# A GCN and a sparse GAT layer on one core: mask bytes in eight row tables in place of mask bits in four, with list rounds and x tiles placed elsewhere

## The chip, the cores and the metric

The kernel runs on one core of one Trainium2 chip. The metric is the device time of one execution in microseconds. Before the change it is 2188.02 us, the median of three runs (2182.11 to 2196.11).

## The reference

There are 4096 nodes with 512 features, all fp32, and a weighted adjacency matrix `adj` in which under one per cent of the entries are non-zero. Two layers are computed, each with a layer norm and a ReLU in front and a residual around it:

```python
# layer 0
h = max(layernorm(x), 0)
d = rowsum(adj) ** -0.5                      # 0 where the sum isn't positive
x = x + relu((d[:, None] * adj * d[None, :]) @ h @ W + b)
# layer 1
h = max(layernorm(x), 0)
g = h @ W1
e = leaky_relu((g @ a[:512]) + (g @ a[512:]).T, 0.2)
pos = softmax(where(adj > 0, e, -1e12), axis=1)
neg = -softmax(where(adj > 0, -e, -1e12), axis=1)
x = x + elu(concat([pos @ h, neg @ h], axis=1) @ wtrans)
```

Layer 1 needs of `adj` only where it is positive: a mask of 4096 x 4096.

## The kernel before

**Layer 0, first pass.** The 4096 source nodes are 32 tiles j of 128 rows. For each j the kernel loads the rows of `adj` (four loads of 512 KB), sums them on ScalarE (ACT) and VectorE (DVE), normalizes the tile of x, turns it by four TensorE (PE) transposes and a copy to `hx_t` (`turn_x`), multiplies it with W (`project`) and scales it to `y0[j]`, which stays in SBUF (`scale`). At the same time it multiplies the first group of six target tiles, 26 to 31, with the `y0[j]` that is there. `turn_x` for tile j + 2 runs in the middle of the matmuls of tile j, and `project` for tile j + 1 stands before those matmuls.

**Layer 0, groups.** Target tiles are handled in groups, `GROUPS`, of which the first is that of the first pass; seven follow, called b = 1 to 7 here: four target tiles each, and two in the last. A group loads tiles `at` of the transposed adjacency (`load_at`, on the queue of SyncE, SP, four buffers), multiplies them with `y0` (`multiply`, line 718) in 16 steps jp of two source tiles each, and accumulates in PSUM. The accumulators of the previous group are taken up at the start of the next (`finish0`, the epilogue).

**Mask bits.** Each tile `at` also passes through `pack` on DVE: line 627 makes of each element either a power of two or zero, line 639 sums 16 of them to a 16-bit word, line 644 reduces the words to a flag for each pair of a source node and a block of 64 targets. Words are kept in SBUF (`words`) until a whole slice of a table is there; then GpSimd (POOL) writes them with one DMA (line 654). Two groups, (24, 2) and (12, 4), are packed ahead of their time with extra loads of their `at` tiles through the same four buffers (`EARLY`): in b = 2, and in b = 4 and 5.

**Epilogue.** For each of its tiles `finish0` computes the layer's output, writes it to DRAM (`x1_dram`), normalizes it to a row `h` (two buffers) and writes `h` with its attention term to four tables in DRAM, two writes on ACT's queue and two on POOL's. There are four tables because each holds, next to the row of every source node, the mask of that node for a quarter of the targets. At its end the attention terms `s_all` are scattered to DRAM and broadcast back to all partitions (`s_bc`), on ACT's queue (lines 693 and 697).

**Lists.** For each block of 64 targets the kernel lists the source nodes with at least one edge into it. DVE finds them in rounds of eight (`list_round`, MAX8 and MATCH_REPLACE8, lines 372 and 374); POOL joins the parts by indirect DMAs (line 387), and SP loads the joined lists as `idx` (`deal`, line 399). The steps of this are queued in `listing`, and the group loop takes two of them in each step jp, and four from b = 6 on.

**Layer 1.** For each of 32 pairs of blocks (128 targets) POOL gathers 22 chunks of 128 table rows (line 861), in three tiles of 8, 6 and 8 chunks; a block of 64 targets uses two of the three. `weights` computes for block r the sums z of both attention terms (line 882), picks the bits of the mask out of the gathered words (line 890), takes the leaky ReLU (899), two exponentials on ACT (902), multiplies them by the mask (903), and sums them. `product` multiplies with the gathered rows (934), and `finish1` applies wtrans (967). The first gathers read the third of the four tables.

The Tile framework places instructions by readiness as well as by program order, except where `keep_in_program_order` (the argument `pin`) holds them.

Of the kernel before, what the change touches and what calls it, by code (L numbers as in the profile page):

```python
# [19 lines left out]
P = 128  # L20
# [9 lines left out]
RB = 64  # L30
WB = 16
NE = 8
CAPS = (168, 144, 168)
NTAB = 4
CHUNKS = (8, 6, 8)
ROW_T = 512
ROW_W = 516
ROW = 548
MAXS = 40.0
# [217 lines left out]
def gcn_gat_kernel(  # L257
# [37 lines left out]
    STR = LEN + 2 * P  # L295
    WPR = RB // WB
    RPT = NR // NTAB
    LOFF = (0, CAPS[0], CAPS[0] + CAPS[1])

# [25 lines left out]

    wts = const.tile([P, WB], U16, name="wts")
    for k in range(WB):
        nc.gpsimd.memset(wts[:, k : k + 1], 1 << k)
    base = const.tile([P, 1], F32, name="base")
# [46 lines left out]
    def table_rows(g, c, lst):  # L376

        li = const.tile([P, CAPS[c]], I32, tag=f"li{c}", name=f"li{g}_{c}")
# [36 lines left out]
    with tc.tile_pool(name="y0", bufs=1) as y_pool, tc.tile_pool(  # L415
# [39 lines left out]
        xs, hx_t, ars, parts, y0 = {}, {}, {}, {}, {}  # L455
        words, packed = {}, {}

# [100 lines left out]
        def turn_x(ln_pool, j, pin=False):  # L558

            hx = ln_pool.tile([P, F], F32, tag="hx", name=f"hx{j}", bufs=2)  # L560
            normalize(hx, xs.pop(j), f"a{j}", pin)
            tp = bank(f"tx{j}")
            for c in range(FC):
                i = nc.tensor.transpose(
                    tp[:, c * P : (c + 1) * P], hx[:, c * P : (c + 1) * P], ident
                )
                if pin:
                    tc.keep_in_program_order(i)
            hx_t[j] = ln_pool.tile([P, F], F32, tag="hx_t", name=f"hx_t{j}")
            nc.vector.tensor_copy(hx_t[j], tp)  # L570
# [47 lines left out]
        def pack(i0, j0, at, pin=False):  # L618

            nj, w = at.shape[1], at.shape[2] // WB  # L620
            g, w0 = i0 * P // (N // NTAB), i0 * P % (N // NTAB) // WB
            if g not in words:
                words[g] = bits_pool.tile(
                    [P, NJ, RPT * WPR], U16, tag="words", name=f"words{g}", bufs=3
                )
            m = bits_pool.tile([P, nj * w, WB], U16, tag="m", name=f"m{i0}_{j0}")
            i = nc.vector.scalar_tensor_tensor(  # L627
                m,
                at.rearrange("p c (w k) -> p (c w) k", k=WB),
                0.0,  # L630
                wts[:, :].unsqueeze(1).to_broadcast([P, nj * w, WB]),
                ALU.is_gt,
                ALU.mult,
            )
            if pin:
                tc.keep_in_program_order(i)
            wd = words[g][:, j0 : j0 + nj, w0 : w0 + w]
            with nc.allow_low_precision("sums of different powers of two below 2**16 are exact"):
                nc.vector.tensor_reduce(  # L639
                    wd, m.rearrange("p (c w) k -> p c w k", c=nj), AX.X, ALU.add  # L640
                )
            e, k = j0 // EJ, j0 % EJ
            half, r = i0 // (NJ // 2), i0 % (NJ // 2) * 2
            nc.vector.tensor_reduce(  # L644
                flags[half].rearrange("p (k e) b -> p k e b", e=NE)[
                    :, k : k + nj, e, r : r + w // WPR
                ],
                wd.rearrange("p c (b w) -> p c b w", w=WPR),
                AX.X,
                ALU.max,  # L650
            )
            packed[g, e] = packed.get((g, e), 0) + nj * w
            if packed[g, e] == EJ * RPT * WPR:
                nc.gpsimd.dma_start(  # L654
                    out=rows_of(g, e)[:, :, ROW_W : ROW_W + RPT * WPR // 2],
                    in_=words[g][:, e * EJ : (e + 1) * EJ, :].bitcast(I32),
                )

        def finish0(work, i0, acc):
# [8 lines left out]
            for j, y in enumerate(ys, i0):  # L668
# [14 lines left out]
                e, k = j // EJ, j % EJ  # L683
                for g in (2, 3, 0, 1):
                    (nc.scalar, nc.gpsimd)[g % 2].dma_start(
                        out=rows_of(g, e)[:, k, :ROW_W], in_=h.bitcast(I32)
                    )
                dot(0, s_all[:, j : j + 1])
                nc.vector.tensor_copy(t_all[:, j : j + 1], h[:, ROW_T : ROW_T + 1])

            n = len(acc)
# [35 lines left out]
        with tc.tile_pool(name="w0", bufs=1) as w0_pool, tc.tile_pool(  # L727
# [23 lines left out]
            for j in range(NJ):  # L751
# [38 lines left out]
        with tc.tile_pool(name="work0", bufs=2) as work:  # L790
            for b, (i0, n) in enumerate(GROUPS[1:], 1):
                acc = None
                for jp in range(NJ // 2):
# [20 lines left out]
                pending = (i0, acc)  # L814
            finish0(work, *pending)


# [25 lines left out]
    def sparse_layer1():  # L843
        with tc.tile_pool(name="wt", bufs=1) as wt_pool, tc.tile_pool(
# [31 lines left out]
            def weights(r):  # L876

                nk = sum(CHUNKS[r % 2 : r % 2 + 2])
                z = tmp.tile([P, nk, RB], F32, tag="z", name=f"z{r}")
                m = tmp.tile([P, nk, RB], U16, tag="m1", name=f"m1_{r}")  # L880
                for gt, k, n in parts(r):
# [4 lines left out]
                        ALU.add,  # L886
                    )
                    w = gt[:, :, ROW_W:].bitcast(U16)
                    w = w[:, :, (r % RPT) * WPR : (r % RPT + 1) * WPR]
                    nc.vector.tensor_tensor(  # L890
                        m[:, k : k + n].rearrange("p k (w c) -> p k w c", c=WB),
                        w.unsqueeze(3).to_broadcast([P, n, WPR, WB]),
                        wts[:, :].unsqueeze(1).unsqueeze(1).to_broadcast([P, n, WPR, WB]),
                        ALU.bitwise_and,
                    )
                p = p_pool.tile([P, nk, 2, RB], F32, tag="p", name=f"p{r}")
                for k, n in ((0, nk),) if r not in first else tuple((k, n) for _, k, n in parts(r)):
                    zk = z[:, k : k + n]
                    nc.vector.scalar_tensor_tensor(zk, zk, ALPHA, zk, ALU.mult, ALU.max)  # L899
                    for g in range(2):  # L900
                        e = p[:, k : k + n, g, :]
                        nc.scalar.activation(e, zk, AF.Exp, scale=(1.0, -1.0)[g])  # L902
                        nc.vector.scalar_tensor_tensor(  # L903
                            e, m[:, k : k + n], 0.0, e, ALU.is_gt, ALU.mult
                        )
                half = nk // 2
# [145 lines left out]
```

## Time and profile before

| | us |
|---|---|
| median of three runs | 2188.02 |
| the profiled execution | 2204.95 |
| its span, first to last instruction | 2203.1 |
| PE busy | 2076.8 |
| DVE busy | 1273.7 |
| POOL busy | 963.5 |
| last matmul of layer 0, start | 1096.52 |
| first gather of layer 1, start | 1109.60 |
| first product of layer 1, start | 1131.50 |

The profile shows one execution. Durations of instructions come from the engines; a matmul's end is modelled, and since matmuls are pipelined a row of them reads as busy even where each takes longer than it must. Each fp32 matmul is two instructions in the counts. "Idle before" a group of instructions is the time its engine stood still just before them, and the name behind the arrow is what ended it. The granted clock of PE is given as a share of full speed. The DMA share is the mean busy share of the 16 DMA engines.

### The profile page before, as it was taken

The numbers are of one execution on the slowest core, as the hardware profiler recorded it, in microseconds if no ns is written. First come the engines' busy times: TensorE is split into PE (matmuls) and PEld (weight loads), VectorE is DVE, ScalarE is ACT, GpSimd is POOL, SyncE is SP. The second block draws the span as 40 slices with busy tenths as digits, with TensorE's granted clock in tenths as the row PEclk, the third lists the DMA queues.
The fourth block names the chain that finished last, engine by engine and source line by source line (L and its number), as shares of the span: only waits on it lengthen the run. The fifth ranks groups of instructions, "written<-read, shape, count | busy, mean of one in ns | idle before, by whom it ended". The sixth has DMA issues, their size and how long they took to land.

```text
span 2203.1 us, 16742 instructions
## 1 busy us (share of the span) xinstructions
PE 2076.8 (94%) x5184; PEld 936.5 (43%) x5184; DVE 1273.7 (58%) x2559; ACT 407.5 (18%) x745; POOL 963.5 (44%) x1009
## 2 busy tenths in 40 slices
PE   7998999999998898999846999999999999999998
PEld 3443444434443343444323444444444444444443
DVE  6665537465899866587235545555554555555451
ACT  5555511000000000000011212122211212221221
POOL 2000002021102231102267777777777777777750
PEclk9999999999999999999968999999999999999999
DMA  9899728273735447452586777777777776777750
GB/s 350 320 345 323 290 69 256 79 210 113 216 88 181 123 145 198 152 152 88 153 257 196 202 214 207 210 208 212 206 207 214 212 212 198 210 212 205 218 162 21
DMA packets 172825, 431.59 MB, mean 196 GB/s; under 512 B 39091, under 2 KB 48307, under 8 KB 172726
## 3 DMA queue, kind: packets, MB, share of 16 engines
q0 software_dynamic: 72144, 243.76, 38.5%
q1 hardware_dynamic: 84112, 164.75, 23.2%
q10 hardware_dynamic: 16470, 21.92, 3.0%
q8 instruction: 42, 0.69, 0.1%
q14 instruction: 57, 0.47, 0.1%
HBM read 376.67 MB, written 53.67 MB: 195 GB/s over the span
## 4 chain that ended last, share of the span: by engine, by line
PE 42%; POOL 3%; issue 2%; DMA 2%; DVE 1%; ACT 0%; DVEq 0%; another core or an unknown queue 0%; POOLq 0%
PE u L934 32%; PE o L967 9%; POOL g L861 3%; PE tp L952 1%; DMA table<-h 1%; DMA g<-table,idx 1%; DMA wt_sb<-in_wtrans 0%; PE cs L923 0%; DVE p L903 0%; DVE z L882 0%; DVE z L899 0%; DVE m L890 0%; DVE total L912 0%; DVE eo L979 0%; DVE eo L975 0%
## 5 line engine op out<-in xcount | busy, mean ns | idle before, releaser
L718 PE MATMUL acc<-y,at 128*128 128x512 f32 x2048 | 903.8, 598 | 34.4 <-DMA at<-in_adj_t 34.2
L861 POOL DMA_INDIRECT g<-table,idx x704 | 796.4, 1131 | 231.4 <-issue 197.7
L934 PE MATMUL u<-g,p 128*128 128x512 f32 x1792 | 792.6, 599 | 28.8 <-DMA g<-table,idx 24.7
L718 PEld LDWEIGHTS acc<-y,at 128*128 128x128 f32 x2048 | 389.0, 192 | 519.6 <-issue 470.9
L934 PEld LDWEIGHTS u<-g,p 128*128 128x128 f32 x1792 | 337.5, 191 | 433.5 <-issue 420.5
L882 DVE TENSOR_TENSOR z<-g,s_bc 128x512 f32<-128x512 f32 (+1 forms) x128 | 80.2, 627 | 456.3 <-DMA g<-table,idx 401.6
L627 DVE SCALAR_TENSOR_TENSOR m<-at,wts 128x1024 uint16<-128x1024 f32 (+2 forms) x144 | 157.8, 1098 | 162.7 <-DMA at<-in_adj_t 162.4
L967 PE MATMUL o<-wt_sb,ut 128*128 128x512 f32 x512 | 226.0, 593 | 2.6 <-issue 2.0
L902 ACT ACTIVATE p<-z 128x896 f32<-128x896 f32 (+2 forms) x132 | 115.1, 919 | 515.1 <-issue 418.3
L639 DVE TENSOR_REDUCE words<-m 128x64 uint16<-128x1024 uint16 (+2 forms) x144 | 157.4, 1095 | 2.2
L903 DVE SCALAR_TENSOR_TENSOR p<-m,p 128x896 f32<-128x896 uint16 (+2 forms) x132 | 134.5, 1060 | 26.4 <-ACT p L902 15.1
L967 PEld LDWEIGHTS o<-wt_sb,ut 128*128 128x128 f32 x512 | 94.7, 190 | 111.0 <-issue 110.3
L595 PE MATMUL yp<-w_sb,hx_t 128*128 128x512 f32 x256 | 122.6, 624 | 19.0 <-DVE flags L644 6.4
L548 ACT ACTIVATE rrb<-rrb 128x1 f32<-128x1 f32 x32 | 6.1, 198 | 668.9 <-DVE rrb L547 447.2
L387 POOL DMA_INDIRECT ld<-li,off x48 | 47.0, 978 | 183.5 <-DVE li L380 89.2
L654 POOL DMA_DIRECT2D table<-words x32 | 24.5, 766 | 224.3 <-DVE flags L644 142.9
L585 ACT ACTIVATE ar<-ar 128x1024 f32<-128x1024 f32 x96 | 100.7, 1050 | 49.9 <-DMA ar<-in_adj 49.4
L556 POOL DMA_DIRECT2D xt<-in_x x28 | 15.3, 547 | 205.8 <-ACT hx L552 99.3
L943 ACT ACTIVATE us<-u,rl 128x512 f32<-128x512 f32 x64 | 43.9, 686 | 246.1 <-issue 118.8
L595 PEld LDWEIGHTS yp<-w_sb,hx_t 128*128 128x128 f32 x256 | 49.5, 199 | 89.3 <-issue 73.0
L912 DVE TENSOR_TENSOR total<-total 128x384 f32<-128x384 f32 (+2 forms) x192 | 81.9, 427 | 2.3
L372 DVE MAX8 lst<-keys 128x8 f32<-128x512 f32 x120 | 79.6, 680 | 0.8
(122 smaller groups left out, 1115.7 us busy)
## 6 DMA issues: line engine op xcount, KB each, us to landing
ar<-in_adj SPq DMA_DIRECT2D x128, 512.0 KB
at<-in_adj_t SPq DMA_DIRECT2D x120, 512.0 KB
table<-h ACTq DMA_DIRECT2D x64, 258.0 KB
table<-h POOLq DMA_DIRECT2D x64, 258.0 KB
at<-in_adj_t SPq DMA_DIRECT2D x32, 384.0 KB
g<-table,idx POOLq DMA_INDIRECT x704
xr<-in_x POOLq DMA_DIRECT2D x32, 256.0 KB
x1d<-y POOLq DMA_DIRECT2D x32, 256.0 KB
```

The costliest lines, as they stand in the source:

```text
L585: i = nc.scalar.activation(ar, ar, AF.Identity, accum_out=part[:, c : c + 1])
L595: nc.tensor.matmul(yp, hx_t[j][:, c * P : (c + 1) * P], w0_sb[:, c, :], start=c == 0, stop=c == FC - 1,)
L627: i = nc.vector.scalar_tensor_tensor(m, at.rearrange("p c (w k) -> p (c w) k", k=WB), 0.0, wts[:, :].unsqueeze(1).to_broadcast([P, nj * w, ...
L639: nc.vector.tensor_reduce(wd, m.rearrange("p (c w) k -> p c w k", c=nj), AX.X, ALU.add)
L718: nc.tensor.matmul(a, at[:, c, it * P : (it + 1) * P], y0[j0 + c], start=j0 + c == 0, stop=j0 + c == NJ - 1,)
L861: nc.gpsimd.indirect_dma_start(out=gt[:, k, :], out_offset=None, in_=table[2 * n // RPT], in_offset=bass.IndirectOffsetOnAxis(ap=idx[n // ...
L882: nc.vector.tensor_tensor(z[:, k : k + n], gt[:, :, ROW_T : ROW_T + 1].bitcast(F32).to_broadcast([P, n, RB]), s_bc[r // 8][:, r % 8 * RB : ...
L902: nc.scalar.activation(e, zk, AF.Exp, scale=(1.0, -1.0)[g])
L903: nc.vector.scalar_tensor_tensor(e, m[:, k : k + n], 0.0, e, ALU.is_gt, ALU.mult)
L912: nc.vector.tensor_tensor(total[:, :n], total[:, :n], total[:, half - n : half], ALU.add)
L934: nc.tensor.matmul(u, p[:, k0 + k].rearrange("p g c -> p (g c)"), gt[:, k, :F].bitcast(F32), start=k0 + k == 0, stop=k0 + k == nk - 1,)
L967: nc.tensor.matmul(po, ut[:, g, c, :], wt_sb[:, g * FC + c, :], start=g == 0 and c == 0, stop=g == 1 and c == FC - 1,)
```

## The change

The mask is kept as one byte for each element. `pack` becomes one comparison that writes bytes and one reduction that reads them as 32-bit words for the flags; the byte tile, four source tiles deep and in two buffers, is the source of the DMA to the table, with no `words` in between. Since a mask of bytes is eight times as large, there are eight tables, each with the mask for an eighth of the targets (512 bytes in each row; a row has 644 words of 4 bytes, before 548), and `finish0` writes `h` eight times: six writes on ACT's queue and two on POOL's. In layer 1 the multiplication by the mask reads the bytes in the gathered row, separately for the two gathered tiles, and the picking of bits goes.

The scatter and broadcast of the attention terms become a function of their own, `spread_s`, on SP's queue, called at step 6 of the next group (for the last group, after its epilogue). The lists take no step in jp 0 to 2 of the groups up to b = 6; later they take two, in b = 6 four, and in b = 7 one in each jp. In the first pass `turn_x` handles tile j + 3 in the matmuls of tile j, from j = 0 on, with four buffers of `hx_t`.

```diff
-NTAB = 4
+NTAB = 8
-ROW = 548
+ROW = 644
...
-            hx_t[j] = ln_pool.tile([P, F], F32, tag="hx_t", name=f"hx_t{j}")
+            hx_t[j] = ln_pool.tile([P, F], F32, tag="hx_t", name=f"hx_t{j}", bufs=4)
...
-            nj, w = at.shape[1], at.shape[2] // WB
-            g, w0 = i0 * P // (N // NTAB), i0 * P % (N // NTAB) // WB
-            if g not in words:
-                words[g] = bits_pool.tile(
-                    [P, NJ, RPT * WPR], U16, tag="words", name=f"words{g}", bufs=3
-                )
-            m = bits_pool.tile([P, nj * w, WB], U16, tag="m", name=f"m{i0}_{j0}")
-            i = nc.vector.scalar_tensor_tensor(
-                m,
-                at.rearrange("p c (w k) -> p (c w) k", k=WB),
-                0.0,
-                wts[:, :].unsqueeze(1).to_broadcast([P, nj * w, WB]),
-                ALU.is_gt,
-                ALU.mult,
-            )
+            nj, w = at.shape[1:]
+            e, k = j0 // EJ, j0 % EJ
+            if k == 0:
+                masks[i0] = bits_pool.tile([P, EJ, w], U8, tag="m", name=f"m{i0}_{j0}")
+            m = masks[i0][:, k : k + nj]
+            i = nc.vector.tensor_scalar(m, at, 0.0, None, ALU.is_gt)
...
-                nc.vector.tensor_reduce(
-                    wd, m.rearrange("p (c w) k -> p c w k", c=nj), AX.X, ALU.add
-                )
...
-                wd.rearrange("p c (b w) -> p c b w", w=WPR),
+                m.bitcast(I32).rearrange("p c (b w) -> p c b w", w=RB // 4),
...
+            if k + nj == EJ:
+                for t in range(i0 // TT, (i0 + w // P - 1) // TT + 1):
+                    a, b = max(i0, t * TT), min(i0 + w // P, (t + 1) * TT)
+                    nc.gpsimd.dma_start(
+                        out=rows_of(t, e)[
+                            :, :, ROW_W + (a - t * TT) * P // 4 : ROW_W + (b - t * TT) * P // 4
+                        ],
+                        in_=masks[i0][:, :, (a - i0) * P : (b - i0) * P].bitcast(I32),
+                    )
...
-                for g in (2, 3, 0, 1):
-                    (nc.scalar, nc.gpsimd)[g % 2].dma_start(
+                for n, g in enumerate((4, 5, 6, 7, 0, 1, 2, 3)):
+                    (nc.scalar, nc.scalar, nc.gpsimd)[n % 3].dma_start(
...
-            nc.scalar.dma_start(out=sd.rearrange("(k p) -> p k", p=P), in_=s_all[:, i0 : i0 + n])
+            nc.sync.dma_start(out=sd.rearrange("(k p) -> p k", p=P), in_=s_all[:, i0 : i0 + n])
...
-                nc.scalar.dma_start(
+                nc.sync.dma_start(
                     out=s_bc[j // 4][:, j % 4 * P : (j % 4 + k) * P],
...
-                turn = partial(turn_x, ln_pool, j + 2, j < 3) if 0 < j < NJ - 2 else None
+                turn = partial(turn_x, ln_pool, j + 3, j < 2) if j < NJ - 3 else None
...
+                    if jp == 6:
+                        spread_s(pending[0], len(pending[1]))
...
-                    for _ in range(2 if b < 6 else 4):
+                    for _ in range((2, 4, 1)[max(b - 5, 0)] if jp > 2 or b > 6 else 0):
...
-                        ALU.bitwise_and,
...
-                        nc.vector.scalar_tensor_tensor(
-                            e, m[:, k : k + n], 0.0, e, ALU.is_gt, ALU.mult
-                        )
+                for gt, k, n in parts(r):
+                    m = gt[:, :, ROW_W:].bitcast(U8)[:, :, r % RPT * RB : (r % RPT + 1) * RB]
+                    for g in range(2):
+                        e = p[:, k : k + n, g, :]
+                        nc.vector.scalar_tensor_tensor(e, m, 0.0, e, ALU.is_gt, ALU.mult)
```

More of the change, by code (lines that the diff above doesn't have):

```diff
@@ L30 @@
 RB = 64
-WB = 16
 NE = 8
 CAPS = (168, 144, 168)
-NTAB = 4
+NTAB = 8
 CHUNKS = (8, 6, 8)
@@ L295, in gcn_gat_kernel @@
     STR = LEN + 2 * P
-    WPR = RB // WB
     RPT = NR // NTAB
+    TT = RPT * RB // P
     LOFF = (0, CAPS[0], CAPS[0] + CAPS[1])
@@ L324, in gcn_gat_kernel @@
     s_bc = [const.tile([P, 4 * P], F32, name=f"s_bc{k}") for k in range(NJ // 4)]
-    wts = const.tile([P, WB], U16, name="wts")
-    for k in range(WB):
-        nc.gpsimd.memset(wts[:, k : k + 1], 1 << k)
     base = const.tile([P, 1], F32, name="base")
@@ L376, in table_rows @@
     def table_rows(g, c, lst):
-        li = const.tile([P, CAPS[c]], I32, tag=f"li{c}", name=f"li{g}_{c}")
+        li = list_pool.tile([P, CAPS[c]], I32, tag=f"li{c}", name=f"li{g}_{c}")
         src = lst[:, LOFF[c] : LOFF[c] + CAPS[c]]
@@ L455, in gcn_gat_kernel @@
         xs, hx_t, ars, parts, y0 = {}, {}, {}, {}, {}
-        words, packed = {}, {}
+        masks = {}
         def make_keys(g):
@@ L618, in pack @@
         def pack(i0, j0, at, pin=False):
-            nj, w = at.shape[1], at.shape[2] // WB
-            g, w0 = i0 * P // (N // NTAB), i0 * P % (N // NTAB) // WB
-            if g not in words:
-                words[g] = bits_pool.tile(
-                    [P, NJ, RPT * WPR], U16, tag="words", name=f"words{g}", bufs=3
-                )
-            m = bits_pool.tile([P, nj * w, WB], U16, tag="m", name=f"m{i0}_{j0}")
-            i = nc.vector.scalar_tensor_tensor(
-                m,
-                at.rearrange("p c (w k) -> p (c w) k", k=WB),
-                0.0,
-                wts[:, :].unsqueeze(1).to_broadcast([P, nj * w, WB]),
-                ALU.is_gt,
-                ALU.mult,
-            )
+            nj, w = at.shape[1:]
[4 more added lines that the diff above has]
+            i = nc.vector.tensor_scalar(m, at, 0.0, None, ALU.is_gt)
             if pin:
                 tc.keep_in_program_order(i)
-            wd = words[g][:, j0 : j0 + nj, w0 : w0 + w]
-            with nc.allow_low_precision("sums of different powers of two below 2**16 are exact"):
-                nc.vector.tensor_reduce(
-                    wd, m.rearrange("p (c w) k -> p c w k", c=nj), AX.X, ALU.add
-                )
-            e, k = j0 // EJ, j0 % EJ
             half, r = i0 // (NJ // 2), i0 % (NJ // 2) * 2
@@ L645, in pack @@
                 flags[half].rearrange("p (k e) b -> p k e b", e=NE)[
-                    :, k : k + nj, e, r : r + w // WPR
+                    :, k : k + nj, e, r : r + w // RB
                 ],
-                wd.rearrange("p c (b w) -> p c b w", w=WPR),
+                m.bitcast(I32).rearrange("p c (b w) -> p c b w", w=RB // 4),
                 AX.X,
@@ L651, in pack @@
             )
[L652 to L656, printed above, removed]
-                )
+            if k + nj == EJ:
[7 more added lines that the diff above has]
+                    )
         def finish0(work, i0, acc):
@@ L689, in finish0, with spread_s @@
                 nc.vector.tensor_copy(t_all[:, j : j + 1], h[:, ROW_T : ROW_T + 1])
-            n = len(acc)
+        def spread_s(i0, n):
             sd = s_dram[i0 * P : (i0 + n) * P]
-            nc.scalar.dma_start(out=sd.rearrange("(k p) -> p k", p=P), in_=s_all[:, i0 : i0 + n])
+            nc.sync.dma_start(out=sd.rearrange("(k p) -> p k", p=P), in_=s_all[:, i0 : i0 + n])
             j = i0
@@ L814, in gcn_gat_kernel @@
                 pending = (i0, acc)
+            while listing:
+                listing.pop(0)()
             finish0(work, *pending)
+            spread_s(pending[0], len(pending[1]))
         ok = small.tile([P, 8], F32, tag="ok", name="ok", bufs=1)
@@ L879, in weights @@
                 z = tmp.tile([P, nk, RB], F32, tag="z", name=f"z{r}")
-                m = tmp.tile([P, nk, RB], U16, tag="m1", name=f"m1_{r}")
                 for gt, k, n in parts(r):
@@ L886, in weights @@
                         ALU.add,
[L887 to L893, printed above, removed]
-                        ALU.bitwise_and,
                     )
@@ L902, in weights @@
                         nc.scalar.activation(e, zk, AF.Exp, scale=(1.0, -1.0)[g])
-                        nc.vector.scalar_tensor_tensor(
-                            e, m[:, k : k + n], 0.0, e, ALU.is_gt, ALU.mult
-                        )
+                for gt, k, n in parts(r):
[3 more added lines that the diff above has]
+                        nc.vector.scalar_tensor_tensor(e, m, 0.0, e, ALU.is_gt, ALU.mult)
                 half = nk // 2
```

## The prediction

> **What bounds the kernel now.** I read the busy shares first, then the windows cut at the matmuls that open each group, then the waits of PE, VectorE (DVE) and SP in each, and last the chain of waits.
>
> ```profile
> PE 2076.8 (94%) x5184; PEld 936.5 (43%) x5184; DVE 1273.7 (58%) x2559; ACT 407.5 (18%) x745; POOL 963.5 (44%) x1009
> ```
>
> Cut at the changes of stage, the windows give 332 us for the first pass (group 26 to 31), 765 for the seven other groups, 78 for the passage to layer 1, 1028 for layer 1. In layer 1 PE is busy 1012.9 of 1028, and the chain is PE alone: one node block takes 32.2 us (product starts at 1245.23, 1277.45, 1309.68). Only the first 1175 us can be shortened. The groups, in order (columns: stretch, length, PE, PEld, DVE, ACT, POOL busy with counts, clock, DMA share, GB/s):
>
> ```profile
> 332.07:441.94 109.87, 109.87 (x257) 48.64 (x256) 63.40 (x125) 5.99 (x12) 14.36 (x31) 1.00 0.55 170
> 441.94:560.60 118.66, 112.59 (x257) 48.74 (x256) 68.86 (x132) 4.07 (x8) 19.12 (x34) 0.99 0.57 158
> 560.60:671.78 111.18, 111.18 (x283) 49.56 (x284) 107.30 (x230) 3.85 (x8) 16.37 (x27) 1.00 0.48 139
> 671.78:799.08 127.30, 113.43 (x257) 48.65 (x256) 102.39 (x190) 3.85 (x8) 34.09 (x45) 0.99 0.51 153
> 799.08:924.05 124.97, 114.78 (x258) 50.22 (x257) 75.44 (x123) 3.96 (x8) 15.67 (x30) 0.95 0.60 168
> 924.05:1035.15 111.10, 111.10 (x284) 49.48 (x283) 99.57 (x256) 3.73 (x8) 20.24 (x33) 1.00 0.46 137
> 1035.15:1096.52 61.37, 57.12 (x128) 24.98 (x127) 13.10 (x46) 3.85 (x8) 18.37 (x30) 0.94 0.56 155
> ```
>
> Group b=1 loses nothing: 109.87 us for 257 matmuls, 0.4275 each. Against that b=2, 4, 5 lose 8.8, 17.4, 15.1 us, b=3 and 6 1.3 and 1.2, b=7 (half a group: 54.9) 6.4: together 50. The losers b=2, 4, 5 are the groups that also load and pack an EARLY group through the same four `at` buffers, so their prefetch reaches about two steps, 13.7 us, not four, 27. All their PE gaps end on "DMA at<-in_adj_t". The worst come just after an epilogue. For b=2:
>
> ```profile
> 468.00:470.00 2.00, 2.00 (x6) 0.92 (x5) 2.00 (x3) 0.00 (x0) 0.26 (x2) 1.00 0.97 293
> 472.00:474.00 2.00, 2.00 (x6) 0.93 (x5) 0.00 (x0) 0.00 (x0) 0.00 (x0) 1.00 0.95 44
> 476.00:478.00 2.00, 0.44 (x2) 0.00 (x0) 0.00 (x0) 0.00 (x0) 0.00 (x0) 1.00 0.64 53
> 480.00:484.00 4.00, 2.90 (x4) 1.31 (x5) 2.92 (x4) 0.00 (x0) 0.00 (x0) 0.68 0.50 111
> ```
>
> The DMA share stays high while the rate falls from 293 to 44 GB/s, for 8 us: the scatter of s_all into DRAM, issued at 466.72 and landed by 478.88 when s_bc is loaded, is many 4-byte writes. The same hole follows the scatters of 712.24, 839.39 and 1105.45. After it the clock is at 0.68. Other losses: DVE is full in b=3 and the start of b=4 (two waits of 1.86 us), and SP, in order, sits in front of the idx loads for the joins (waits of 13 and 20 us, before 797.51 and 1080.25).
>
> First pass: projections start 9.62 us apart from 48.2 to 269.5, then 9.02. The excess, 23 x 0.6 = 14 us, stands in PE's waits of 60 to 270 us as waits for rra, hx, hx_t, rs and flags: late turns.
>
> **What the Trainium skill says.** The Trainium skill, VectorE: DVE Perf Modes, "The perf-mode tier table": fp32 tensor_scalar from SBUF runs at 2x, tensor_reduce at 1x. The trace agrees: 512 elements cost 420 ns as TENSOR_SCALAR (one<-keys), 680 as a two-input operation; no row has a byte output. DMA: Bandwidth & Descriptors, "Specifications": below 512 B a transfer is read-modify-write. The 8 us hole fits, though the trace doesn't show the cause. SBUF — State Buffer, "Who interferes with whom": a DVE instruction with two SBUF inputs contends with a GpSimd one that reads SBUF. Gathers last 0.95 us alone, 1.3 to 1.8 beside such DVE work, which agrees.
>
> **Pack.** Columns: form, count, busy, mean ns, idle before.
>
> ```profile
> L627 DVE SCALAR_TENSOR_TENSOR m<-at,wts 128x1024 uint16<-128x1024 f32 x96 | 116.8, 1217 | 141.1 <-DMA at<-in_adj_t 141.0
> L639 DVE TENSOR_REDUCE words<-m 128x64 uint16<-128x1024 uint16 x96 | 116.3, 1212 | 1.4
> L644 DVE TENSOR_REDUCE flags<-words 128x16 f32<-128x64 uint16 x96 | 20.4, 212 | 1.4
> L483 DVE TENSOR_SCALAR one<-keys 128x512 f32<-128x512 f32 x6 | 2.5, 420 | 0.0
> ```
>
> A pack of 1024 columns costs 2.64 us. After: one TENSOR_SCALAR, an estimate from the same page of the Trainium skill (2x, some 150 fixed cycles and 0.96 GHz, "Side-by-side"): (512 + 150) / 0.96 = 690 ns (bounds 690 and, at 1x, 1217), and a flags reduction over 256 words, 212 + 192 x 1.04 = 412 ns (slope from L639 and L644). So 1.10 us (to 1.63); saved 1.54 x 96, and likewise 1.19 x 32 and 0.84 x 16: 199 us of DVE (at least 110). PE waits for little of it. I count back: the two waits in b=4 with their slack, 4 us; two fifths, my choice, of what b=2, 4, 5 lose, since `at` buffers are freed by packs 1.5 us sooner and the list rounds stand clear of steps 0 to 2: 16 of 41. Groups: **-20** (bounds -35 and +30).
>
> **h tables.** Eight writes of 258 KB per block for four: +128 x 264 kB = 33.8 MB. Issue: ACT 64 to 192 times 0.42 us, idle 82% and so nothing; POOL stays at 64. Four blocks take 8.3 MB, about 24 us at 350 GB/s instead of 12, more beside loads. It lies under 109 us of matmuls; if that cover is thin, it is in b=2, 4, 5: in the bound above. The zero rows (+4 x 0.51 us on POOL near 16 us) cost nothing.
>
> **Mask DMAs.** 72 for 32 on POOL, +40 x 0.757 = 30 us, POOL being idle 80% there; 16.8 MB for 2.1. New wait: the byte tile has two buffers and is freed only when its DMA has landed, so a pack can wait for POOL's queue. I take 0 where one stream packs; bounds 0 and 15 us per two-stream epilogue (rival C).
>
> **Scatter of s moved** from ACT to SP: 7 scatters and 9 broadcasts, behind the loads of step 6 and ahead of later ones. ACT loses a wait it didn't feel. SP now waits for s_all (DVE) and then for the scatter, about 10 us, and later `at` loads queue behind. With full buffers at step 6 that is hidden; I take 0, bounds -8 and +8 a two-stream group.
>
> **Turned sooner.** One more tile of lead: **-10** of the 14 us (bounds -14, +3). DMA allows it: loads ended by 260, at 346 GB/s.
>
> **Passage to layer 1.**
>
> ```profile
> 1109.60 1.01 POOL L861 DMA_INDIRECT g<-table,idx  x1 [3.60 <-DMA table<-h]
> 1127.25 0.69 DVE L882 TENSOR_TENSOR z<-g,s_bc 128x512 f32<-128x512 f32 x1 [20.28 <-DMA g<-table,idx]
> ```
>
> Gathers start once table 2 has landed. After, block 25's write to table 4 stands behind six of block 24's in ACT's queue: 1.6 MB at some 216 GB/s (60% of 360) is 7.3 us where two stood before (2.4), and SP's scatter now makes its hole in these writes. First gather +9 us; but earlier gathers lay in the hole until 1118, so z moves +5. POOL, at 1.25 us a gather, carries +9 to the block that PE awaits at 1174. Two dropped m operations (685 and 550 ns) take back 1. **+8** (bounds -2, +15).
>
> **Layer 1.** m goes (128 instructions, 79 us); the multiply splits by part, 124 x 1089 ns becoming 248 of 688 and 548: +18. DVE is half idle: nothing. Rows of 2576 B for 2192: a POOL gather of 946 ns median costs no more for bytes, as a join of 16 rows of 672 B costs 978. 22 x 1.43 = 31.5 us of POOL in a block of 32.2 is tight, but fewer two-input DVE operations help. DMA share 0.72 would be about 0.84. **-1** (bounds -5, +12).
>
> **Sum**: -10 - 20 + 8 - 1 = -23. The profiled execution, 2203.1 span and 2204.95 in all, lies 17 us above the median of 2188.02; taken off that median: **2165**, own range 2140 to 2185.
>
> **Rivals.** B, the wait only changes its name: bursts twice as long keep `at` late (groups 0), and x tiles, for which DVE already waits 55.5 us, arrive no sooner for earlier turns (-2). With -4 for DVE's help in b=4, +8 and -1: +1, so 2189. For: rates of 350 in epilogues. Against: b=1, 3, 6 hide theirs entirely. C, slower: in b=2, 4, 5 two mask streams share two buffers; POOL, held before its h MEMSET by doubled writes (waits of 11.6 us now), issues a mask late, DVE stops at the next tile, no `at` buffer comes free. At 15 us a group, with the slow clock, +45, with +8, -10 and -1: +42, so 2230. It decides once mask landing takes over 13.7 us, the prefetch. Against: POOL has 80% idle.
>
> **Chances**: forecast 0.52, B 0.20, C 0.28. Faster by over 1% (below 2166; 1% is about what this kernel's spread of 2182 to 2196 lets one tell): 0.34 + 0.03 = 0.37; within 1%: 0.18 + 0.15 + 0.04 = 0.37; slower: 0.02 + 0.24 = 0.26. Range 2140 to 2225, leaving out a tenth on each side.
>
> **What would show it.** Right: groups b=2, 4, 5 at 110 to 118 us, no PE wait for rra or hx_t in the first pass, pack near 1.1 us, first gather 5 to 10 us after its distance now (13 us after the last dense matmul). Wrong: TENSOR_SCALAR near 1.2 us; DVE waits for table<-m; SP waits before the scatter with PE gaps behind; node blocks longer than 32.2 us.

## The result and the profile after

| | before | after |
|---|---|---|
| median, us (4 runs each) | 2189.67 (2182.11 to 2196.11) | 2258.45 (2255.03 to 2260.73) |
| ratio after / before, 95% interval | | 1.0314 [1.0278, 1.0351] |
| span of the profiled execution | 2203.1 | 2257.0 |
| first pass (start of b = 1) | 332.1 | 336.4 |
| groups b = 1 to 7 | 764.4 | 814.3 |
| last dense matmul to first product | 35.0 | 46.6 |
| first product to end | 1071.6 | 1059.7 |

The change costs 69 us, 93 above the forecast and 33 above the upper end of the range. The loss is in the seven groups (+50) and in the passage to layer 1 (+12, taken back by a shorter layer 1). Engine by engine nothing looks wrong. From the page of the changed kernel, the busy shares:

```profile
PE 2082.3 (92%) x5184; PEld 941.8 (42%) x5184; DVE 1036.6 (46%) x2411; ACT 401.2 (18%) x745; POOL 928.4 (41%) x1037
```

DVE has 237 us less to do. Cut by groups, the windows (stretch, length, then busy times, clock, DMA share, GB/s) show where PE stopped:

```profile
336.44:455.88 119.44, 111.82 (x257) 49.20 (x256) 38.70 (x107) 5.76 (x12) 20.52 (x39) 0.97 0.73 227
455.88:582.16 126.28, 112.22 (x258) 49.07 (x257) 42.51 (x112) 3.74 (x8) 20.21 (x35) 0.95 0.68 206
582.16:693.26 111.10, 111.10 (x284) 49.48 (x283) 89.08 (x231) 3.83 (x8) 21.58 (x35) 1.00 0.61 186
693.26:844.32 151.06, 120.43 (x257) 51.56 (x256) 63.98 (x148) 3.85 (x8) 35.20 (x50) 0.89 0.64 187
844.32:963.87 119.55, 112.50 (x258) 49.51 (x257) 38.64 (x94) 3.74 (x8) 18.70 (x33) 0.97 0.69 216
963.87:1075.60 111.73, 111.16 (x283) 49.48 (x282) 96.20 (x250) 3.74 (x8) 18.12 (x31) 1.00 0.59 174
1075.60:1150.69 75.09, 57.30 (x129) 24.98 (x127) 16.53 (x52) 3.74 (x8) 20.96 (x33) 0.86 0.69 184
```

b = 1, which lost nothing before, now loses 9.6 us against its 109.87; b = 2 loses 16 (before 9), b = 4 and b = 7 lose 41 and 20. Only b = 5 gained (5 us), and b = 3 and 6 stand where they stood. SP's queue tells what happens in the losers. First its waits (line, what it waited for: total, times, longest), then its instructions around the scatter in b = 1 and in b = 4:

```profile
SPq L690 <- DMA at<-in_adj_t: 171.1, 38, 10.1
SPq L682 <- DMA sd<-s_all: 83.0, 8, 14.1
SPq L690 <- DMA table<-h: 66.7, 9, 17.6
SPq L678 <- DMA table<-h: 31.4, 5, 11.1
SPq L678 <- DVE t_all L673: 16.4, 4, 9.1
```

```profile
385.46 0.37 SPq L678 DMA_DIRECT2D sd<-s_all  x1
398.46 0.81 SPq L682 DMA_DIRECT2D s_bc<-sd  x2
399.37 2.72 SPq L690 DMA_DIRECT2D at<-in_adj_t  x4
```

```profile
756.51 0.37 SPq L678 DMA_DIRECT2D sd<-s_all  x1
756.97 0.52 SPq L690 DMA_DIRECT2D at<-in_adj_t  x1
768.38 0.34 SPq L682 DMA_DIRECT2D s_bc<-sd  x1
771.22 0.89 SPq L690 DMA_DIRECT2D at<-in_adj_t  x2
```

L678 is the scatter and L682 the broadcast in `spread_s`; L690 is `load_at`. In b = 1 the hold is plain: SP stands until the scatter has landed, 13 us after its issue, and then four loads go out at once, so that all four buffers had been free. PE, which had stopped at 398.40, goes on when the first of them lands, at 406.02.

In b = 4 SP also stands ahead of the scatter, from 740 us on:

```profile
SPq L678 <- DVE t_all L673: 9.1, 1, 9.1
SPq L678 <- DMA table<-h: 7.1, 1, 7.1
```

One load slips in behind the scatter, then SP stands until the scatter has landed, 11.9 us after its issue. What the DMA engines do meanwhile (windows of 2 us, last two columns DMA share and GB/s; a share above 1 comes of packets that start in a window and end after it):

```profile
756.00:758.00 2.00, 2.00 (x6) 0.95 (x5) 0.55 (x3) 0.00 (x0) 1.48 (x4) 1.00 0.69 238
760.00:762.00 2.00, 0.00 (x0) 0.00 (x0) 0.00 (x0) 0.00 (x0) 0.00 (x0) 1.00 2.02 34
762.00:764.00 2.00, 0.00 (x0) 0.00 (x0) 0.00 (x0) 0.00 (x0) 0.00 (x0) 1.00 0.63 10
766.00:768.00 2.00, 0.00 (x0) 0.00 (x0) 0.00 (x0) 0.00 (x0) 0.00 (x0) 0.50 0.76 40
768.00:770.00 2.00, 0.00 (x0) 0.00 (x0) 0.00 (x0) 0.00 (x0) 0.00 (x0) 0.50 0.95 319
```

For six microseconds next to nothing moves, though the engines read as busy; when the scatter has landed, 319 GB/s return. PE's clock has gone to 0.50 by then. From the timeline, the first `pack` and the first matmul after it:

```profile
770.49 0.69 DVE L621 TENSOR_SCALAR m<-at 128x1024 uint8<-128x1024 f32 x1 [13.94 <-DMA at<-in_adj_t]
775.65 4.64 PE L703 MATMUL acc<-y,at 128*128 128x512 f32 x5 [16.46 <-DMA at<-in_adj_t]
```

The load that slipped in lands only behind the scatter, at 770.47, after 13.5 us (the page's median is 4.4). The next load, at 771.22, waits for the pack of that tile (until 771.20), not for the broadcast alone. By this reading the loss in b = 4 is made of SP's stand ahead of the scatter and of the slow transfer beside it, more than of the hold behind it. Full buffers would have carried PE for 27 us; here it stopped 2.7 us after the scatter. In b = 1, 2 and 5 it stops 9 to 13 us after one, for 7.6, 13.0 and 7.1 us. In b = 7 SP had first waited for a write of `h` (17.6 us) and for the joins (`deal`, 15.6), and PE stood already; the load that came out at 1127.83, behind the scatter of 1126.13, took 13.8 us to land. PE stood 17.8 us.

### The profile page after: what moved, and what is told of

It is laid out like the page before. It is cut to its first block, busy times and chain, and to the rows that moved or that the text cites. A ratio compares the mean times of both kernels' runs of the same rounds, so it can differ in the third digit from the quotient of the medians.

```text
span 2257.0 us, 16899 instructions
## 1 busy us (share of the span) xinstructions
PE 2082.3 (92%) x5184; PEld 941.8 (42%) x5184; DVE 1036.6 (46%) x2411; ACT 401.2 (18%) x745; POOL 928.4 (41%) x1037
## 5 line engine op out<-in xcount | busy, mean ns | idle before, releaser
L703 PE MATMUL acc<-y,at 128*128 128x512 f32 x2048 | 910.1, 602 | 77.1 <-DMA at<-in_adj_t 77.1
L851 POOL DMA_INDIRECT g<-table,idx x704 | 729.5, 1036 | 291.0 <-issue 183.7
L621 DVE TENSOR_SCALAR m<-at 128x1024 uint8<-128x1024 f32 (+2 forms) x144 | 90.8, 631 | 339.4 <-DMA at<-in_adj_t 298.3
L636 POOL DMA_DIRECT2D table<-m x72 | 55.0, 765 | 356.5 <-DVE m L621 312.7
L888 DVE SCALAR_TENSOR_TENSOR p<-g,p 128x512 f32<-128x512 uint8 (+1 forms) x256 | 143.1, 620 | 65.7 <-ACT p L883 65.6
L370 DVE MATCH_REPLACE8 keys<-lst,keys 128x512 f32<-128x512 f32 x114 | 76.1, 669 | 0.0
```

Source lines behind the costliest of these rows:

```text
L621: i = nc.vector.tensor_scalar(m, at, 0.0, None, ALU.is_gt)
L703: nc.tensor.matmul(a, at[:, c, it * P : (it + 1) * P], y0[j0 + c], start=j0 + c == 0, stop=j0 + c == NJ - 1,)
L851: nc.gpsimd.indirect_dma_start(out=gt[:, k, :], out_offset=None, in_=table[2 * n // RPT], in_offset=bass.IndirectOffsetOnAxis(ap=idx[n // ...
L888: nc.vector.scalar_tensor_tensor(e, m, 0.0, e, ALU.is_gt, ALU.mult)
```

## The experiments

The leading theory: the scatter's place on SP's queue holds the loads, and eight writes of `h` make it land later. Its rivals: the eight writes alone; the mask's two buffers (rival C); the sooner turn taking PSUM banks in the first pass. Every ratio below is to the kernel before on the same chip, with its 95% interval; group lengths come from one profile each, and profiles of kernels that differ in the first pass alone vary by 1 to 5 us in the groups (745.3 and 743.3, 764.4 and 759.1, 814.3 and 818.5). Where `h` goes to four tables, half of the writes are left out and the gathers take the mask bytes of other blocks.

**The scatter back on ACT**, with its broadcast, behind the epilogue as before the change:

```diff
-            nc.sync.dma_start(out=sd...
+            nc.scalar.dma_start(out=sd...
...
                         finish0(work, *pending)
+                        spread_s(pending[0], len(pending[1]))
...
-                    if jp == 6:
-                        spread_s(pending[0], len(pending[1]))
```

> The changed kernel with the scatter and broadcast of s back on ACT's queue, called right behind the epilogue. Queue theory (SP holds the at loads while it waits for the scatter to land): groups b=1, 2, 4, 7 fall back by 9, 5, 15 and 8 us, the time to about 2215, ratio to the kernel before 1.01. Write theory (the 33.8 MB of doubled table writes delay the at loads wherever the scatter stands): 2245 to 2260, and the gaps stay. Hole theory (the 4-byte writes stop all DMA for 8 us wherever they are issued): a part comes back, 2225 to 2240, and PE still waits 4 us or more behind each scatter in b=2, 4, 5.

Measured: 1.0155 [1.0094, 1.0216]; groups 784.2, b = 1 at 109.9 and b = 2 at 118.2 again, b = 4 still 143.0 and b = 7 71.2. So half of the loss is the place of the scatter, and half is not; b = 4 and 7 give back 8 and 4 us of the 15 and 8 expected.

**The scatter on SP in the kernel before**, with its broadcast, nothing else of the change:

```diff
-            nc.scalar.dma_start(out=sd...
+            nc.sync.dma_start(out=sd...
+                    if jp == 6:
+                        spread_s(pending[0], len(pending[1]))
```

> The kernel before with one part of the change: scatter and broadcast of s on SP, at step 6 of the next group. Queue theory: slower than before by 15 to 35 us, ratio 1.007 to 1.016, with SP waiting 10 to 13 us for each of eight scatters. Write and hole theories: within 5 us of the kernel before.

Measured: 1.0084 [1.0062, 1.0107]; groups 784.3, of which b = 5 has 136.1. SP waits 78.7 us for the scatter there, nearly as much as in the changed kernel (83.0), for half the cost: 0.8 points against the 1.6 between the run above and the change.

**`h` to four tables only**, with the scatter on SP and, in a second kernel, on ACT:

```diff
-                for n, g in enumerate((4, 5, 6, 7, 0, 1, 2, 3)):
-                    (nc.scalar, nc.scalar, nc.gpsimd)[n % 3].dma_start(
+                for n, g in enumerate((0, 1, 2, 3)):
+                    (nc.scalar, nc.gpsimd)[n % 2].dma_start(
...
-                        in_=table[2 * n // RPT],
+                        in_=table[2 * n // RPT % 4],
```

> The changed kernel with h written to four tables only, two writes on ACT and two on POOL for each tile; the gathers read those four, so the rows hold masks of other blocks and the output isn't the reference's; work and bytes of layer 1 stay. Write theory: about 2205, gaps in b=1, 2, 4, 7 gone. Queue theory: the scatter lands sooner, since fewer writes stand in front, but SP still waits 8 us or more for each: 2235. Hole theory: 2235 to 2245, with the passage about 10 us shorter.

> The changed kernel with h written to four tables (masks read in layer 1 are those of other blocks, as in e3_half) and the scatter of s on ACT: the fourth corner of two by two. The seven groups took 814 us with eight writes and SP, 784 with eight and ACT, 771 with four and SP. If the two costs simply add: 741, the floor of PE being 714. If they are one (the scatter lands late because the writes stand in front, and SP waits for it): 760 to 771. Median about 2200.

Measured: 1.0130 [1.0043, 1.0217] on SP and 1.0028 [1.0010, 1.0047] on ACT; groups 771.3 and 768.2. Both causes together account for the loss. By the group lengths they are in part one cost, as the expectation of 760 to 771 has it: SP adds 30 us with eight writes and 3 with four (20 in the kernel before). By the ratios SP adds 1.0 points with four writes too, but in that profile they don't stand where the scatter is: the first product starts at 1145.58 us with SP and at 1146.20 with ACT, and layer 1, after the last scatter, takes 1088.6 us against 1059.9. Its first block takes 73 us there, 43 in the run with ACT, with a DVE wait of 34 us whose cause the profile does not name.

What may join the two shows in b = 1. The hold on SP is the same, 10.8 us with eight writes and 11.0 with four. With eight, SP has waited 24.7 us for writes of `h` shortly before, and the group takes 119.4 us; with four it has waited 4.8, and the group takes 111.8. That the first wait uses up the cover of the second is argued from these lengths.

**Four mask buffers** for two:

```diff
-                masks[i0] = bits_pool.tile([P, EJ, w], U8, tag="m", name=f"m{i0}_{j0}")
+                masks[i0] = bits_pool.tile([P, EJ, w], U8, tag="m", name=f"m{i0}_{j0}", bufs=4)
```

> The changed kernel with four buffers for the byte mask tile in place of two. Mask theory (rival C of the prediction): DVE's 41 us of waits for table<-m go and b=4 gets shorter by 12 us or more, 2240. Queue theory: the waits go, the time stays within 5 us, since the at loads are held on SP.

Measured: 1.0299 [1.0274, 1.0323], the changed kernel's ratio. DVE's waits for the mask's DMAs fell from 40.7 us to 2.3, so the wait of rival C was there; PE's waits for `at` stayed at 84.7 (77.1 with two buffers), and b = 4 took 154.7 us. Taking it out shortens nothing beside the scatter on SP. In the kernel with nothing scattered further down DVE still waits 26.5 us for these DMAs in b = 4; whether they cost time there is not tried.

**The turn put back** to tile j + 2, with the buffers of `hx_t` that it had before:

```diff
-            hx_t[j] = ln_pool.tile([P, F], F32, tag="hx_t", name=f"hx_t{j}", bufs=4)
+            hx_t[j] = ln_pool.tile([P, F], F32, tag="hx_t", name=f"hx_t{j}")
...
-                turn = partial(turn_x, ln_pool, j + 3, j < 2) if j < NJ - 3 else None
+                turn = partial(turn_x, ln_pool, j + 2, j < 3) if 0 < j < NJ - 2 else None
```

> The changed kernel with x tiles turned when they were before (j + 2, three buffers). Bank theory (a tile turned sooner takes one of the two PSUM banks that six accumulators leave, so the next projection waits for ACT's y): first pass from 336 back to 328 us or less, no PE wait for ACT y, time down by 6 to 10. Lead theory, that of the prediction (a tile turned sooner saves waits): first pass 340 or more, time up.

Measured: 1.0336 [1.0316, 1.0356], not separable in time from the change. In the profile the first pass is 342.5 us for 336.4, and PE's waits for the projections (60 to 300 us) change their name. First the turn put back, then the changed kernel:

```profile
PE yp L591 <- DVE rra L542: 19.1, 7, 4.2
PE yp L591 <- DVE hx_t L566: 1.3, 3, 0.7
```

```profile
PE yp L591 <- ACT y L612: 14.7, 7, 3.6
```

The sooner turn removes the waits for late turns, as intended, and gives some 6 us, not 10: PE then waits for ACT's scaling of the projection before. That wait is the one that the rival on banks named, but it costs less than the waits that went, so as a cause of the loss this rival is out.

**3.1 MB of extra writes in the first pass of the kernel before**, as many bytes as the mask of group 26 to 31 has:

```diff
                 pack(i0, j, ats.pop(j), j < 2)
+                if j % 2:
+                    nc.gpsimd.dma_start(out=more[j // 2], in_=rank[:, :384])
```

> The kernel before with 3.1 MB of additional writes in the first pass (16 DMAs of 197 kB from POOL, as much as the byte masks of the first group), that nobody reads. Byte theory (the first pass is near the limit of the transfers, so the mask bytes are why it is 4 us longer in the changed kernel in spite of the earlier turn): first pass 340 us or more. If the transfers are covered: within 2 us of 332, and the longer first pass comes from elsewhere.

Measured: 1.0006 [0.9988, 1.0024]; the first pass 337.7 us for 332.1 in its profile. That is between the 340 of the one expectation and the 332 of the other. Bytes alone may lengthen the first pass by such an amount (it took 329.8 to 333.3 us in the other variants of the kernel before with the later turn), but the total doesn't show it, so this one stays a reading of single profiles.

**No scatter at all.** If `s_bc` is made on the chip, both the 4-byte writes and the hold on SP go. Three forms were tried. The first two copy a column of `s_all` to a tile `sw` and turn that on PE; the first with ACT's copy in the changed kernel (called at step 9), and with DVE's in the kernel before (at step 12):

```diff
+                sp = bank(f"sp{j}")
+                for t in range(k):
+                    sw = small.tile([P, P], F32, tag="sw", ...)
+                    nc.scalar.activation(sw, ones, AF.Copy, scale=s_all[:, j + t : j + t + 1])
+                    nc.tensor.transpose(sp[:, t * P : (t + 1) * P], sw, ident)
+                nc.scalar.copy(s_bc[j // 4][:, j % 4 * P : (j % 4 + k) * P], sp[:, : k * P])
```

> The changed kernel without the trip of s through DRAM: s_bc is made by PE transposes of columns that ACT spread, so there is no scatter, no broadcast load and no wait on SP. Queue theory: as e1, about 2215. Hole theory: lower than e1 by 10 us or more, about 2195, since the 8 us in which the DMA moves little are gone, in the passage to layer 1 too (first product 36 us after the last dense matmul at most, now 47). Write theory: 2240 or more.

> The kernel before with s_bc made by DVE, PE transposes and an ACT copy at step 12 of the next group, no scatter through DRAM. Hole theory: groups b=2, 4, 5 from 119, 127, 125 to about 112, 117, 115, the passage shorter by 6 us: 25 to 35 us faster than the kernel before, ratio 0.985 to 0.989. If the hole only filled time that at loads or DVE would have lost anyway: within 5 us.

Measured: 1.0085 [1.0062, 1.0108] for the changed kernel and 0.9952 [0.9936, 0.9968] for the one before. In the first PE waited 13.8 and 16.4 us for ACT's copies, behind writes of `h` that ACT was still issuing.

The second form serves each group's columns one group later, when they have long been there (with DVE's copy; in the kernel before, in the changed one, and in the kernel before with the sooner turn and three buffers of `hx_t`):

```diff
-                    if jp == 6:
-                        spread_s(pending[0], len(pending[1]))
+                    if jp == 6 and b > 1:
+                        spread_s(*GROUPS[b - 2])
```

> The kernel before with s_bc made on chip as in b2_pe, but one group later (step 6 of the group after next, the last two after the loop), so that no engine waits for s_all. b2_pe spent 29 us of PE waits on its own transposes. Hole theory: these go and nothing takes their place, seven groups about 735 us, ratio 0.980 to 0.986. If the waits only hid late at loads: groups stay at 755 to 761, ratio 0.993 to 0.997.

> The changed kernel with the same: no scatter, no broadcast load, s_bc one group later. What is left against b4_pe_late is the rest of the change: eight writes, byte masks, list rounds, earlier turn. Queue theory with the write theory (eight writes alone cost 16 us in the groups where no load waits on SP): seven groups 750 to 760 us, b=4 still the longest at about 135 since the idx loads wait in it, passage 38 to 40, ratio 1.000 to 1.006. If eight writes cost nothing once SP is free: groups 740, ratio 0.990.

> b4_pe_late with x tiles turned one tile sooner (j + 3, three buffers of hx_t). Lead theory (e4_turn: without the sooner turn the first pass of the changed kernel is 6 us longer): first pass from 332 to 322 to 326, 6 to 10 us less than b4_pe_late. If the first pass is held by the transfers: within 2 us of b4_pe_late.

Measured: 1.0030 [1.0009, 1.0052], 1.0301 [1.0270, 1.0333] and 0.9997 [0.9974, 1.0020]. The first two are misses, in the groups too (763.5 us for 735, 809.6 for 750 to 760); the second is as slow as the change with no scatter in it. In the third the sooner turn gave 4.3 us in the first pass (325.6 for 329.9), for 6 to 10. PE's waits in the second kernel show why:

```profile
PE sp L684 <- DVE sw L683: 62.5, 11, 19.4
PE u L918 <- DMA g<-table,idx: 25.1, 2, 24.1
```

The column was there, the copy of it was not. DVE's timeline ahead of the longest of these waits:

```profile
772.66 0.69 DVE L621 TENSOR_SCALAR m<-at 128x1024 uint8<-128x1024 f32 x1 [9.66 <-DMA at<-in_adj_t]
773.39 0.42 DVE L625 TENSOR_REDUCE flags<-m 128x16 f32<-128x256 int32 x1
773.73 0.28 DVE L683 TENSOR_SCALAR sw<-ones,s_all 128x128 f32<-128x128 f32 x1
```

DVE runs in order as well, and the copy stood behind a pack that waited for `at`: PE waited until 774.06, 19.4 us in all. The change had put the loads behind SP's wait; this experiment put PE behind DVE's. It priced its own copy.

The third form, called at step 12, needs no copy: the transpose reads the column repeated along the free axis.

```diff
+                    col = s_all[:, j + t : j + t + 1].to_broadcast([P, P])
+                    nc.tensor.transpose(sp[:, t * P : (t + 1) * P], col, ident)
```

> The kernel before with s_bc made on the chip and nothing scattered, as in the run with DVE's copies (0.995), but the transposes read a column of s_all repeated along the free axis, so that no tile sw is made on DVE and PE waits for none; step 12, SP has no part in it. If the 27 to 29 us that PE waited for sw in that run are the price of the copies and of their place on DVE's queue: seven groups at 730 to 740 us (760.8 with the copies, floor 714), 0.980 to 0.987 of the kernel before. If those waits only stood where waits for `at` tiles would stand otherwise: 755 to 765 us and 0.994 to 0.998.

> The changed kernel with nothing scattered and no sw. If the scatter on SP and its hold on the loads are 30 us of the loss and PE's waits for sw were what spoiled the two runs with transposes (1.0085 and 1.030): seven groups at 745 to 760 us, 0.996 to 1.004, and no group but the fourth over 120. If eight writes of h hold the loads back by themselves: seven groups at 780 or more and 1.01 and more.

> The changed kernel with nothing scattered, no sw, and h written to four of the eight tables (the gathers read the mask bytes of another block). Against the run with all eight writes this prices the writes alone: 8 to 16 us less in the groups and about 7 less in the passage, 0.986 to 0.994, if the writes are a cost of their own; the same time within 5 us if they cost only together with the scatter.

> The same with tiles of x turned one step of the loop sooner (three buffers of hx_t). By the run that undid the turn (6 us): first pass 4 to 7 us shorter than without it, 0.977 to 0.984. If the sooner turn is worth nothing where the writes are four: as without it.

Measured: the kernel before 0.9915 [0.9881, 0.9948], groups 745.3; with the sooner turn 0.9860 [0.9826, 0.9893]; the changed kernel 1.0027 [1.0017, 1.0037], groups 766.6; the changed kernel with four writes 0.9854 [0.9820, 0.9889], groups 731.1. The first missed its 0.980 to 0.987, and groups of 730 to 740, by a little: b = 4 and 5 keep waits for `at` of 2 to 3 us each. The sooner turn missed its 0.977 to 0.984 too, with 3.3 us in the first pass (326.5 for 329.8) for 4 to 7. The changed kernel lies within its 0.996 to 1.004, but its groups are 7 us over the 745 to 760; the writes alone cost 35 us in the groups for the 8 to 16 expected. Where these 35 lie, which was open, the windows of b = 4 and b = 7 show. With eight writes:

```profile
671.94:814.86 142.92, 118.41 (x262) 51.54 (x261) 54.39 (x128) 4.54 (x9) 33.49 (x48) 0.89 0.61 196
1038.27:1103.48 65.21, 57.28 (x132) 25.34 (x131) 16.07 (x51) 4.32 (x9) 20.45 (x33) 0.95 0.64 207
```

and with four:

```profile
669.50:791.46 121.96, 114.23 (x261) 50.02 (x260) 49.15 (x118) 4.44 (x9) 29.28 (x44) 0.97 0.60 190
1013.31:1068.25 54.94, 54.94 (x132) 24.52 (x131) 13.14 (x46) 4.43 (x9) 19.38 (x31) 1.00 0.56 168
```

21 and 10 us of the 35 are in these two; b = 1, 2, 3, 5 and 6 differ by 4 together. SP's queue has a wait that tells the two kernels apart, that of `load_at` (L689 here) for writes of `h`. In the whole run, first with eight writes, then with four:

```profile
SPq L689 <- DMA table<-h: 106.2, 15, 17.6
```

```profile
SPq L689 <- DMA table<-h: 5.0, 2, 4.3
```

A load of `at` needs nothing of these writes. The instruction records tell why it waits: all DMAs of SP and ACT count their landings on the same eight semaphores in turn (POOL's have eight others), and in the kernel with eight writes each of these 15 waits is for the very semaphore that the load is to use next. The load goes out when the write ahead of it on that semaphore has landed. In b = 4 this takes 25.8 us and in b = 7 17.6 us (none in either with four writes), and in both the wait for the joins follows on SP. In b = 7, with eight writes:

```profile
SPq L689 <- DMA table<-h: 17.6, 1, 17.6
SPq L395 <- DMA ld<-li,off: 15.3, 1, 15.3
```

The other groups have such waits too (31.1 us in b = 1, 18.0 in b = 6), but there the buffers cover them. b = 4 also packs a second stream, and its loads wait longer for packs (35.3 us, 17.9 with four writes). So the writes reach the loads by SP's queue. Whether the bytes cost anything besides is not tried: for that all eight writes would have to go out on POOL.

**All of it in one table** (ratio to the kernel before, and in brackets the length of the seven groups in us; the rest of the change is in both right-hand columns; the runs are of several chips):

| scatter of s | kernel before | changed, four writes | changed, eight writes |
|---|---|---|---|
| none | 0.9915 (745.3) | 0.9854 (731.1) | 1.0027 (766.6) |
| on ACT | 1 (764.4) | 1.0028 (768.2) | 1.0155 (784.2) |
| on SP | 1.0084 (784.3) | 1.0130 (771.3) | 1.0314 (814.3) |

Eight writes add 1.7, 1.3 and 1.8 points in the three rows; SP in place of ACT adds 0.8, 1.0 and 1.6 in the three columns; any scatter on ACT costs 0.9, 1.7 and 1.3 over none. With intervals of 0.1 to 0.9 to each side these ratios fit two costs that add. They fit the joint cost of the group lengths as well, 27 us or 1.2 points of SP with eight writes over SP with four, for the ratios give 0.6 there, with about 1.1 to each side. How far the two are one is open. The rest of the change is worth -0.6 without a scatter and +0.3 with one on ACT: little, and of either sign.

Of the kernels that compute the whole reference, the best is the kernel before with the repeated column and the sooner turn: 0.9860, 2164.8 us.

## Why the prediction was wrong

The sum failed in the groups. Along one path through the profiles the seven groups go 764.4, 745.3 (scatter taken out of the kernel before), 731.1 (the rest of the change, with four writes), 766.6 (eight writes), 814.3 (scatter on SP): -19, -14, +35, +48.

- **Scatter on SP: the step that failed.** "With full buffers at step 6 that is hidden; I take 0, bounds -8 and +8 a two-stream group." The wait was foreseen and its length behind the scatter was right ("about 10 us" against 10.4 on the mean, 83.0 / 8); the stand ahead of it was named and not sized (in the groups 31.4 us for writes of `h` and 16.4 for DVE's `t_all`). Wrong was the cover: in b = 1 all four buffers stood empty when the hold ended. I had counted two steps of prefetch for a two-stream group and then let buffers be full just behind an epilogue, when loads are late; and I bounded only two-stream groups. Of these b = 2 and b = 4 lost 8 us each against the scatter on ACT, the bound itself; b = 1, a single stream, lost 9.5 (109.9 to 119.4), and b = 7 lost 4 (71.2 to 75.1). Against the scatter on ACT, the comparison that the step was about, it is 1.0314 against 1.0155: some 35 us.
- **h tables: the second.** "It lies under 109 us of matmuls" is true of five groups to within 4 us and false of b = 4 and b = 7: 35 us in the groups and 8 in the passage, about 38 by the ratios (1.0027 against 0.9854). I averaged the bytes over a group and saw no link between ACT's queue and the loads, where SP's loads wait for the landing of the writes (106.2 us in all with nothing scattered, 5.0 with four writes), and those of a few steps have no slack for it.
- **Groups, -20.** Without a scatter and with four writes the rest of the change does bring 14 (745.3 to 731.1), but with the scatter on ACT it brings none (764.4 to 768.2), so the gain forecast held only where the scatter didn't stand in its way. DVE's relief is right as sized; the two forms and their means from the page by form:

```profile
L621 DVE TENSOR_SCALAR m<-at 128x1024 uint8<-128x1024 f32 x96 | 66.4, 692 | 295.7 <-DMA at<-in_adj_t 255.0 <-DMA table<-m 40.7
L625 DVE TENSOR_REDUCE flags<-m 128x16 f32<-128x256 int32 x96 | 39.8, 415 | 2.4
```

  692 and 415 ns against 690 and 412. The estimate from the Trainium skill's page VectorE: DVE Perf Modes holds for a byte output too.
- **Turned sooner, -10.** Some -3 to -6 in three pairs of profiles. The excess that it was to work on was miscounted: from 48.2 to 269.5 us lie 22 intervals, of 10.06 us, so 23 us and not 14, and the gain was a smaller share of it than was taken. In the first pass the term was outweighed: +4 in sum, so about +10 from elsewhere in that pass. Mask DMAs were taken at 0 "where one stream packs"; 3.1 MB for 0.4 at the 346 GB/s that I had read there are 8 us, which fits and isn't shown.
- **Passage, +8.** +11.6, from 35.0 to 46.6, by the mechanism named and by one more. ACT's issues, the first gather and the first product of the changed kernel:

```profile
1156.97 16.32 ACTq L669 DMA_DIRECT2D table<-h  x12
```

```profile
1179.75 1.02 POOL L851 DMA_INDIRECT g<-table,idx  x1 [19.62 <-DMA x<-x1d]
```

```profile
1197.26 3.75 PE L917 MATMUL u<-g,p 128*128 128x512 f32 x4 [36.33 <-DMA g<-table,idx]
```

  The first gather starts 29 us after the last dense matmul (13 before), for the +9 forecast. With the scatter on ACT it starts 21 us after it: the writes alone are the +8 or so. Twelve writes keep ACT for 16.3 us, but 8.2 of these lie between the issues at 1163.76 and 1171.96, where the next write was to use the semaphore of the scatter on SP's queue, which landed at 1171.94. The passage is 40.8 us with the scatter on ACT, and with nothing scattered 40.2 for eight writes and 32.1 for four.
- **Layer 1, -1.** A block takes 32.22 us before and after. The 12 us by which this profile is shorter prove nothing by themselves: over all runs the stretch from the first product to the end varied from 1059.3 to 1088.6 us, nearly all of it in the first blocks. On the one chip that ran several kernels with each form of layer 1 it took 1059.3 to 1059.9 us in five with bytes and 1063.9 to 1065.0 in three with bits, so some 5 us less.
- **Rivals.** C had the right sign and the wrong wait; four buffers show it. B's burst of writes is the second cause, but it cost time where B only saw a gain vanish, and it reached the loads by SP's queue. No rival put the price at the queue that loads `at`, though the list of what would show the prediction wrong named it: "SP waits before the scatter with PE gaps behind".

## What to carry to other kernels

A DMA whose wait is a round trip through DRAM belongs on no queue that also feeds the bounding engine, unless the buffers of that queue are shown to be full at that very step. Extra transfers are to be held against the tightest stretch of loads, not against the mean of a stage, and the loads' queue is to be read for waits on transfers that the loads have nothing to do with: here two queues that share semaphores waited for each other. And an experiment that takes a wait away by a detour over another engine prices that engine's queue as well: two runs here said "the scatter doesn't matter" until the copy was gone.

## What the runs showed of the hardware

- A scatter of 512 elements of 4 bytes keeps everything else nearly still: 10 and 12 GB/s at DMA shares of 0.5 to 0.6 in b = 4 (762 to 766 us), 3 to 4 GB/s at shares of 0.66 and more in b = 7. It isn't that nothing else was asked for. In the run with four writes and the scatter on ACT two loads were issued within 1.2 us behind the scatter of 715.32, which landed at 727.74; they took 16.2 us, against a median of 4.3 in that run:

```profile
at<-in_adj_t SPq DMA_DIRECT2D x2, 512.0 KB, 16.2
```

- Taking the scatter out of the kernel before gave 0.85% without any other change.
- A transpose that reads one column repeated 128 times takes 273 ns (the median of 32 in the kernel before with nothing scattered), the same as one of a real tile (273 on the mean, `tp`): the broadcast needs no copy ahead of it.
